# Order of the first statistics and the queues of the last table writes in the preparation of a two-layer metaformer kernel

## The chip, the cores and the metric

The kernel runs on one core of a Trainium2 chip. The metric is the device time of one execution in microseconds (us), as the median over runs. The profile is of one further execution.

## What is computed

The input `x` has shape (4, 256, 64, 64), float32. Two layers follow one another, and each adds a convolution branch and then a recurrent branch to `x`:

```python
x = x + dcnv2(ln_c(x), w_off, b_off, w_conv)   # layer 0: 27 offset/mask maps by a 3x3 convolution,
                                               # 9 bilinear samples per pixel, 256x256 weights per tap
t = t + lstm(ln_t(t), ...)                     # along the 4096 tokens, four gates, h and c of 256
x = x + channel_gate(ln_c(x), ...)             # layer 1: x times a sigmoid gate per image and channel
t = t + lstm(ln_t(t), ...)                     # same recurrence with other weights
```

The deformable convolution reads the normalized image at data-dependent places. The kernel serves these reads from a table in DRAM, whose entry for a pixel place holds neighbouring pixels, so that one indirect DMA fetches the corners of 128 samples.

## The kernel before, in words

Everything is float32. A tile is `[128 partitions, 256 channels]`: 4 images times 32 rows of pixels, for one column and one parity of the row (even or odd). There are 128 such tiles, 64 columns times two parities. The on-chip array `ring` takes the even tiles of the preparation and `squares` the odd ones; both hold 40 tiles.

**Preparation** (`prepare`, line 91). The 64 columns are worked in N = 17 groups: one of 2 columns, three of 4, one of 3, one of 5, ten of 4 and a last one of 2. For each group `g`:

- `load` fetches the raw tiles of `x` (groups 0 to 2 through the queues of SyncE and ScalarE, the others through GpSimd's, lines 330 to 335 and 370);
- `stats(g)` computes mean and variance on VectorE (`bn_stats`, then `norm_of`, a Newton iteration of small dependent instructions);
- `norm` normalizes in place on ScalarE;
- `to_table(g)` (line 275) writes the normalized tiles to the DRAM table. For each parity there are four DMAs, one for each image. Before the change the even half (`table<-ring`) is issued by SyncE and the odd half (`table<-squares`) by GpSimd;
- `turned` transposes on TensorE, `taps` and `offsets` make the offset convolution, and `samples` on VectorE turns the offsets into a **plan**: the addresses and the four weights of every sample, kept in DRAM in 16 pieces of 180 KB by GpSimd (`keep`).

`offsets` uses the matrices `from_above` and `from_below`, which are copies of the identity shifted by one row. Before the change they are made in `metaformer_kernel` (lines 1773 to 1778), outside the hand-written order. From group 3 on one weight load (an "errand": `wconv`, then `Us`, `Vs`, `bs` of each gate) goes to SyncE's queue for each group.

**Order.** The class `Ordered` (line 409) wraps an engine so that its instructions keep program order on that engine. All of its instructions show as L420, the helper's line. What is issued through the plain `tc.nc` is placed by the scheduler of the build. Each queue works its instructions in order: a DMA whose data is ready still waits behind the one issued before it on the same engine.

**Sampling and first recurrence** (`sample_and_recur`, line 571). `plan_of` (line 608) fetches a piece of the plan through SyncE's queue when it is first needed (`used<-plan`). `gather` (line 616) issues the indirect DMAs through GpSimd (`squares<-table,used`), 1,152 in all. A gather depends on its plan piece and on the whole table. ScalarE scales the first corner, VectorE adds the other three, TensorE transposes and multiplies with `wconv` (`acc`). From slot 38 of this loop on, the steps of the first recurrence are interleaved with it by a planner with fixed costs. `fetch` (line 686) brings `x` back into `ring` through SyncE's queue.

The first two plan pieces that are read are pieces 14 and 15, since the order starts with the odd tiles of columns 48 to 63; they are written early in the preparation. The class `Gate` (line 1350) makes some accumulators at its start (`gmx`, `lanes`, `own`, lines 1362 to 1370). The second recurrence (`gated_lstm`) follows with the gate between.

Of the kernel before, what the change touches and what calls it, by code (L numbers as in the profile page):

```python
# [11 lines left out]
F32 = mybir.dt.float32  # L12
# [7 lines left out]
P = 128  # L20
B, C, H, W = 4, 256, 64, 64
# [9 lines left out]
R = H // 2  # L31
# [59 lines left out]
def prepare(tc, pools, const, wts_, x_in, table, errands):  # L91
# [3 lines left out]
    after = pools["after"]  # L95
    nc = Ordered(tc.nc, after)
    ident, from_above, from_below = const
# [20 lines left out]
    plan = pools["dram"].tile([NTILE // OC, P, 5, OC, K], F32, name="plan")  # L118
# [104 lines left out]
    N = len(groups)  # L223
# [17 lines left out]
    def columns(e, g, lo, hi):  # L241
        return cols[e][:, at[g] + lo : at[g] + hi]
# [32 lines left out]
    def to_table(g):  # L275

        c, n = groups[g]
        lo, hi = int(g == 0), n + more[g]
        for e, engine in enumerate((nc.sync, nc.gpsimd)):
            if c + n == W:  # L280
                nc.gpsimd.memset(columns(e, g, n, n + 1), 0.0)
            if g == 0:
                nc.gpsimd.tensor_copy(again[:, e], columns(e, 0, 0, 1)[:, 0])
            elif at[g] == 1:
                last = groups[g - 1][1] + more[g - 1]
                nc.gpsimd.tensor_copy(columns(e, g, -1, 0), columns(e, g - 1, last - 1, last))
            if g == N - 1:
                nc.gpsimd.tensor_copy(columns(e, g, n, n + 1)[:, 0], again[:, e])
            for i in range(B):
                rows = tabs[i, :, 1 + e : 1 + H : 2].rearrange("x y c -> y x c")  # L290
                own = columns(e, g, lo - 1, hi)[i * R : (i + 1) * R]
                both = bass.AP(own.tensor, own.offset, [own.ap[0], [C, hi - lo], [1, 2 * C]])
                engine.dma_start(rows[:, c + lo : c + hi], both)
# [44 lines left out]
    stats(0)  # L338
    norm(0, 4)
    to_table(0)  # L340
    xt = turned(*(columns(e, 0, 0, 1)[:, 0] for e in range(2)))
    stats(1)
    stats(2)
# [227 lines left out]
def sample_and_recur(  # L571
# [12 lines left out]
    nc = Ordered(tc.nc, pools["after"])  # L584
# [23 lines left out]
    def plan_of(c):  # L608
        if c not in chunk:
            chunk[c] = stp.tile([P, 5, OC, K], F32, name=f"used{c}", tag="used", bufs=3)  # L610
            nc.sync.dma_start(chunk[c], plan[c])
        return chunk[c]

    rounds = {}
# [735 lines left out]
class Gate:  # L1350
# [3 lines left out]
    def __init__(self, tc, pools, const, params):  # L1354
        self.tc, self.pools, self.const, self.params = tc, pools, const, params
        kp = pools["keep"]
        nc = tc.nc
        self.low = kp.tile([P, NTILE], F32, name="glow", tag="glow")
        self.rs = kp.tile([P, NTILE], F32, name="grs", tag="grs")

        self.mx = kp.tile([P, 2, C], F32, name="gmx", tag="gmx")
        nc.vector.memset(self.mx, -3.0e38)

        self.lanes = kp.tile([P, 2, 2, C], F32, name="lanes", tag="lanes")
        nc.vector.memset(self.lanes, 0.0)
        self.pq = None

        self.own = kp.tile([P, B], F32, name="own", tag="own")
        ident = const[0]
        nc.vector.tensor_reduce(self.own, ident.rearrange("p (i r) -> p i r", i=B), AX.X, ALU.add)  # L1370
# [364 lines left out]
@with_exitstack  # L1735
def metaformer_kernel(ctx: ExitStack, tc: tile.TileContext, a: dict, out: bass.AP):
    nc = tc.nc
    fp = ctx.enter_context(tc.tile_pool(name="flag", bufs=1))
    dr = ctx.enter_context(tc.tile_pool(name="dram", bufs=1, space=DRAM))

    cnt = fp.tile([P, 2, 2], F32, name="cnt")
    x1 = dr.tile([P, NTILE, C], F32, name="x1d")
    x2 = dr.tile([P, NTILE, C], F32, name="x2d")
    ffn = [[[a[f"L{layer}_ffn_{kind}_{g}"] for g in "ioc"] for kind in "UVb"] for layer in range(2)]
    gate = [a[f"L1_conv_{n}"] for n in ("w", "gamma", "beta", "running_mean", "running_var")]

    with ExitStack() as main:

        def pool(name, bufs, space=None):
            kw = {} if space is None else {"space": space}  # L1750
            return main.enter_context(tc.tile_pool(name=name, bufs=bufs, **kw))

        cp = pool("const", 1)
        pools = {
            "chunk": pool("chunk", 2),
            "v": pool("v", 4),
            "small": pool("small", 2),
            "state": pool("state", 1),
            "cm": pool("cm", 6),
            "y": pool("y", 2),  # L1760
            "keep": pool("keep", 1),
            "median": pool("median", 1),
            "dram": dr,
            "tr": pool("tr", 2, PSUM),
            "acc": pool("acc", 2, PSUM),
            "misc": pool("misc", 1, PSUM),
            "ga": pool("ga", 1, PSUM),
            "gb": pool("gb", 1, PSUM),
        }
        ident = cp.tile([P, P], F32, name="ident")  # L1770
        make_identity(nc, ident)

        from_above = cp.tile([P, P], F32, name="from_above")
        nc.vector.tensor_copy(from_above[:, 1:], ident[:, : P - 1])
        nc.vector.memset(from_above.rearrange("p (i r) -> p i r", i=B)[:, :, 0:1], 0.0)
        from_below = cp.tile([P, P], F32, name="from_below")
        nc.vector.tensor_copy(from_below[:, : P - 1], ident[:, 1:])
        nc.vector.memset(from_below.rearrange("p (i r) -> p i r", i=B)[:, :, R - 1 : R], 0.0)
        const = (ident, from_above, from_below)
        pools["ring"] = cp.tile([P, RING, C], F32, name="ring")  # L1780

        pools["squares"] = cp.tile([P, RING, C], F32, name="squares")
        pools["numbers"] = lambda table: table.rearrange("e (c a) -> (e c) a", a=1)
        pools["after"] = InOrder(tc)

        woff = cp.tile([P, NC, K * NOM], F32, name="woff")
        pools["w_off"] = a["w_off"].rearrange("(n p) k o -> p n (k o)", p=P)
        bias = cp.tile([P, NOM], F32, name="bias")
        nc.sync.dma_start(bias, a["b_off"].rearrange("(a o) -> a o", a=1).to_broadcast([P, NOM]))
        wconv = cp.tile([P, NC, K, C], F32, name="wconv")  # L1790
        table = dr.tile([B * NENT, 2 * C], F32, name="table")
        w_conv = a["w_conv"].rearrange("(n p) k o -> p n k o", p=P)
        errands = [[lambda nc: nc.sync.dma_start(wconv, w_conv)], []]
        weights = [lstm_weights(nc, cp, *ffn[n], tag=n, errands=errands[n]) for n in range(2)]
        plan, rest = prepare(
            tc, pools, const, (woff, bias, (a["grid"], a["first"])), a["x"], table, errands[0]
        )
        ws = cp.tile([P, NC, 3], F32, name="ws")
        nc.sync.dma_start(ws, gate[0].rearrange("(k p) u -> p k u", p=P))
        vec = []  # L1800
        for name, v in zip(("gamma", "beta", "rmean", "rvar"), gate[1:]):
            t = cp.tile([P, NC], F32, name=name)
            with nc.allow_non_contiguous_dma(reason="256 numbers"):
                nc.sync.dma_start(t, v.rearrange("(k p) -> p k", p=P))
            vec.append(t)
        gamma, beta, rmean, rvar = vec
        nc.vector.tensor_scalar(rvar, rvar, 1e-5, None, ALU.add)
        scale = cp.tile([P, NC], F32, name="scale")
        nc.vector.tensor_mul(scale, gamma, inv_sqrt(nc, pools["small"], rvar, NC))
        gt = Gate(tc, pools, const, (ws, scale, rmean, beta))  # L1810
        held = sample_and_recur(
            tc, pools, const, wconv, a["x"], table, plan, x1, x2, weights[0], cnt[:, 0], gt, rest, errands[1]
        )
        gated_lstm(tc, pools, const, weights[1], x2, out, cnt[:, 1], gt.gates(held))


    held = fp.tile([P, 1], F32, name="held")
    nc.vector.tensor_reduce(held, cnt.rearrange("p l i -> p (l i)"), AX.X, ALU.add)
    bad = fp.tile([P, 1], F32, name="bad")
    all_held = 4.0 * NC * B * (R - 1)  # L1820
    nc.vector.tensor_scalar(bad, held, all_held - 0.5, None, ALU.is_lt)
    anybad = fp.tile([P, 1], F32, name="anybad")
    nc.gpsimd.partition_all_reduce(anybad, bad, P, bass_isa.ReduceOp.max)
    flag = fp.tile([P, 1], I32, name="flag")
    nc.vector.tensor_copy(flag, anybad)
    again = nc.values_load(flag[0:1, 0:1], min_val=0, max_val=1)
    with tc.If(again > 0):
        in_order(tc, x1, out, ffn, gate)
# [53 lines left out]
```

## Time and profile before

| | |
|---|---|
| three runs | 3296.19, 3307.12, 3334.37 us, median 3307.12 |
| profiled execution | 3307.03 us, span 3305.2 us, 0.967 of the TensorE clock granted |
| busy over the span | PE 93%, DVE 79%, ACT 62%, POOL 49% |
| first table write on SyncE's queue | issued at 19.96 us |
| last table write on SyncE's queue | issued at 189.95 us |
| first gather on GpSimd | issued at 195.30 us |
| first multiplication with `wconv` | 208.77 us |

PE is TensorE's matmul, PEld its weight load, DVE VectorE, ACT ScalarE, POOL GpSimd. SPq, ACTq and POOLq are queues of DMA issues. In a row of the timeline the columns are start and duration in us, engine, line, operation, written tile, read tiles, shape and number of merged instructions; in brackets stands the idle time before it and what ended it. A row of the table of windows gives the stretch and its length, then the busy time of each engine with the number of instructions, the granted clock, the busy share of the 16 DMA engines, and GB/s.

### The profile page before, as it was taken

To read this page: it belongs to the slowest core of one execution; us is meant where nothing else is said; L and a number is where in the kernel's file an instruction comes from. 1 tells how busy PE (TensorE), PEld (TensorE's weight loads), DVE (VectorE), ACT (ScalarE), POOL (GpSimd) and SP (SyncE) were. 2 spreads that over 40 slices of the span, in tenths; PEclk is the share of its full clock that TensorE was granted. 3 is DMA by queue.
4 is the path that set the end of the run, shared out by engine and by line. 5 is a ranking of instruction groups with operands and counts; after the bars stand their busy time and mean duration, and the time that the engine had idled before them with its cause. 6 is when DMAs were issued, how large, how long until landed. Compare 5 with 4: busy or idle time off the path is not lost.

```text
span 3305.2 us, 61505 instructions
## 1 busy us (share of the span) xinstructions
PE 3060.9 (93%) x20382; PEld 2837.9 (86%) x20382; DVE 2622.9 (79%) x7456; ACT 2058.2 (62%) x5446; POOL 1619.8 (49%) x1583
## 2 busy tenths in 40 slices
PE   7956899999999999999999999999894999999998
PEld 6945788898898889999899899988883999999997
DVE  6656778787898889989889889987576677777774
ACT  5734555565676666766676666766774666666663
POOL 3357566666676666766666756664000022222221
PEclk9978999999999999999999999999996999999999
DMA  9997888898889889999899899886102144544442
GB/s 297 332 310 286 296 301 301 287 322 309 320 301 330 302 292 334 322 323 327 306 321 337 294 328 331 309 315 243 49 27 83 56 134 147 153 151 151 150 141 85
DMA packets 317351, 826.57 MB, mean 250 GB/s; under 512 B 104472, under 2 KB 109976, under 8 KB 312160
## 3 DMA queue, kind: packets, MB, share of 16 engines
q0 software_dynamic: 188416, 669.68, 58.2%
q1 hardware_dynamic: 128464, 152.60, 13.8%
q8 instruction: 164, 2.69, 0.3%
q14 instruction: 163, 1.34, 0.1%
q10 hardware_dynamic: 144, 0.26, 0.0%
HBM read 701.46 MB, written 120.94 MB: 249 GB/s over the span
## 4 chain that ended last, share of the span: by engine, by line
PE 79%; issue 9%; ACT 4%; DVE 3%; another core or an unknown queue 2%; DMA 1%; SPq 1%; POOL 0%; ACTq 0%; DVEq 0%; POOLq 0%
PE acc L420 27%; PE ga L420 12%; PE gacc L420 7%; PE gtr L420 7%; PE tr L420 7%; PE gb L420 6%; PE ggb L420 4%; PE gga L420 4%; ACT v L420 1%; PE zacc L420 1%; DMA squares<-table,used 1%; DVE v L420 1%; PE xt L420 1%; PE zga L420 1%
## 5 line engine op out<-in xcount | busy, mean ns | idle before, releaser
L420 POOL DMA_INDIRECT squares<-table,used x1152 | 1373.3, 1192 | 733.4 <-issue 168.5
L420 DVE SCALAR_TENSOR_TENSOR v<-squares,used,v 128x256 f32<-128x256 f32 x3456 | 1412.7, 477 | 132.8 <-ACT v L420 95.6
L420 PE MATMUL acc<-wconv,vt 128*128 128x256 f32 x4608 | 1125.4, 388 | 86.8 <-ACT vt L420 61.5
L420 PEld LDWEIGHTS acc<-wconv,vt 128*128 128x128 f32 x4608 | 849.5, 195 | 194.7 <-ACT vt L420 68.2
L420 ACT COPY vt<-tr 128x512 f32<-128x512 f32 x576 | 335.7, 583 | 710.2 <-PE tr L420 514.0
L420 ACT ACTIVATE v<-squares,used 128x256 f32<-128x256 f32 x1152 | 528.8, 512 | 67.4 <-DMA squares<-table,used 56.9
L420 PE MATMUL tr<-ident,v 128*128 128x128 f32 x2304 | 352.4, 275 | 28.5 <-DVE v L420 23.0
L420 PEld LDWEIGHTS tr<-ident,v 128*128 128x128 f32 x2304 | 276.7, 142 | 44.1 <-DVE v L420 21.3
L420 DVE TENSOR_TENSOR tg<-tg,ti 128x256 f32<-128x256 f32 x284 | 119.9, 422 | 232.2 <-ACT ti L420 222.2
L420 PEld LDWEIGHTS ga<-cm,Us 128*128 128x128 f32 x2272 | 275.1, 193 | 24.8 <-ACT cm L420 16.8
L420 PE MATMUL ga<-cm,Us 128*128 128x128 f32 x2272 | 279.4, 276 | 14.1 <-ACT cm L420 12.4
L420 PEld LDWEIGHTS ga<-h,Vs 128*128 128x128 f32 x2256 | 278.4, 195 | 11.3 <-issue 4.7
L420 PE MATMUL ga<-h,Vs 128*128 128x128 f32 x2256 | 281.6, 278 | 3.7 <-issue 3.6
L420 POOL DMA_DIRECT2D hd<-sqh x60 | 34.8, 580 | 408.5 <-DVE sqh L420 388.0
L420 POOL DMA_DIRECT2D ring<-hd x240 | 144.4, 630 | 166.7 <-DMA hd<-sqh 152.7
L420 DVE TENSOR_TENSOR h<-to,th 128x256 f32<-128x256 f32 x282 | 119.1, 422 | 132.1 <-ACT th L420 118.6
L420 ACT ACTIVATE tg<-gacc,bs 128x128 f32<-128x128 f32 x284 | 88.7, 363 | 185.6 <-PE gacc L420 185.6
L420 PEld LDWEIGHTS gacc<-h,Vs 128*128 128x128 f32 x1128 | 147.5, 192 | 14.7 <-DVE h L420 7.4
L420 PEld LDWEIGHTS gb<-h,Vs 128*128 128x128 f32 x1128 | 148.4, 193 | 10.5 <-issue 4.2
L420 PE MATMUL gacc<-h,Vs 128*128 128x128 f32 x1128 | 150.1, 276 | 6.2 <-DVE h L420 6.2
L420 PEld LDWEIGHTS gb<-cm,Us 128*128 128x128 f32 x1136 | 147.6, 192 | 9.3 <-issue 1.9
L420 PE MATMUL gb<-h,Vs 128*128 128x128 f32 x1128 | 150.8, 276 | 3.7 <-issue 3.7
(219 smaller groups left out, 4551.4 us busy)
## 6 DMA issues: line engine op xcount, KB each, us to landing
squares<-table,used POOLq DMA_INDIRECT x1152
ring<-x2d SPq DMA_DIRECT2D x18, 1024.0 KB
ring<-in_x_dram SPq DMA_DIRECT2D x65, 256.0 KB
x1d<-ring SPq DMA_DIRECT2D x64, 256.0 KB
x2d<-ring SPq DMA_DIRECT2D x16, 1024.0 KB
xd<-sqx SPq DMA_DIRECT2D x64, 256.0 KB
cm<-xd SPq DMA_DIRECT2D x256, 64.0 KB
out_dram<-ring SPq DMA_DIRECT2D x32, 512.0 KB
```

What stands on the lines that cost most here:

```text
L420: ins = op(*args, **kw)
```

## The change

It has four parts, all at the preparation or right after it.

1. In `prepare`, the shifted copies of the identity are made after `stats(0)`, `norm(0, 4)` and `to_table(0)`, inside the hand-written order.
2. In `to_table`, the even half of the last three groups (14, 15, 16) is issued by GpSimd in place of SyncE. These are 12 DMAs.
3. In `plan_of`, the first two plan pieces are fetched through ScalarE's queue in place of SyncE's.
4. In `Gate`, the accumulators at its start join the hand-written order, which puts them after the preparation's VectorE work.

```diff
@@ to_table
-        for e, engine in enumerate((nc.sync, nc.gpsimd)):
+        for e, engine in enumerate((nc.sync if g < N - 3 else nc.gpsimd, nc.gpsimd)):
@@ prepare
     stats(0)
     norm(0, 4)
     to_table(0)
+
+    nc.vector.tensor_copy(from_above[:, 1:], ident[:, : P - 1])
+    nc.vector.memset(from_above.rearrange("p (i r) -> p i r", i=B)[:, :, 0:1], 0.0)
+    nc.vector.tensor_copy(from_below[:, : P - 1], ident[:, 1:])
+    nc.vector.memset(from_below.rearrange("p (i r) -> p i r", i=B)[:, :, R - 1 : R], 0.0)
     xt = turned(*(columns(e, 0, 0, 1)[:, 0] for e in range(2)))
@@ plan_of
-            nc.sync.dma_start(chunk[c], plan[c])
+            (nc.sync if len(chunk) > 2 else nc.scalar).dma_start(chunk[c], plan[c])
@@ Gate.__init__
-        nc = tc.nc
+        nc = Ordered(tc.nc, pools["after"])
@@ metaformer_kernel
-        from_above = cp.tile([P, P], F32, name="from_above")
-        nc.vector.tensor_copy(from_above[:, 1:], ident[:, : P - 1])
-        ...
-        nc.vector.memset(from_below.rearrange("p (i r) -> p i r", i=B)[:, :, R - 1 : R], 0.0)
+        from_above, from_below = (cp.tile([P, P], F32, name=n) for n in ("from_above", "from_below"))
```

More of the change, by code (lines that the diff above doesn't have):

```diff
@@ L1771, in metaformer_kernel @@
         make_identity(nc, ident)
-        from_above = cp.tile([P, P], F32, name="from_above")
[L1774 to L1777, printed above, removed]
-        nc.vector.memset(from_below.rearrange("p (i r) -> p i r", i=B)[:, :, R - 1 : R], 0.0)
+        from_above, from_below = (cp.tile([P, P], F32, name=n) for n in ("from_above", "from_below"))
         const = (ident, from_above, from_below)
```

## The prediction, made before the changed kernel was run

> **What bounds the kernel now.** I read the page first, for the chain that ended last, then the table of windows over the preparation and after it, then the timeline of VectorE at the start and of the two DMA-issuing queues at the end. All parts of the change lie before 196 us, so I need what bounds that stretch and whether a gain there lasts.
>
> ```profile
> PE 79%; issue 9%; ACT 4%; DVE 3%; another core or an unknown queue 2%; DMA 1%; SPq 1%; POOL 0%; ACTq 0%; DVEq 0%; POOLq 0%
> ```
>
> SPq is 1% of the chain: about 33 us at most can be had from SyncE's queue.
>
> ```profile
> 15.00:35.00 20.00, 12.40 (x44) 9.24 (x44) 18.99 (x95) 9.05 (x19) 9.08 (x19) 0.91 1.00 378
> 35.00:80.00 45.00, 43.70 (x271) 40.45 (x272) 28.72 (x110) 34.10 (x72) 15.17 (x29) 1.00 0.92 257
> 80.00:155.00 75.00, 75.00 (x469) 69.82 (x468) 55.48 (x225) 54.34 (x113) 26.84 (x49) 1.00 1.01 336
> 155.00:195.00 40.00, 28.48 (x180) 26.42 (x178) 17.83 (x63) 15.32 (x33) 9.60 (x18) 0.91 0.95 272
> 200.00:220.00 20.00, 12.02 (x51) 9.50 (x52) 14.93 (x36) 8.49 (x17) 15.43 (x18) 0.70 1.01 379
> ```
>
> The last two columns are the DMA share and GB/s. Two things are full at once: the matmul row (75.00 of 75 us from 80 to 155) and the 16 DMA engines (1.01). In 35 to 80 and 155 to 195 the DMA engines have a little idle time and move fewer bytes per us. After 200 they are full again, with gathers.
>
> ```profile
> 13.05 0.28 POOL masks.py:199 TENSOR_SCALAR_AFFINE_SELECT ident<-ident 128x128 f32<-128x128 f32 x1 [9.91 <-issue]
> ...
> 13.36 0.23 DVE L1774 COPY from_above<-ident 128x127 f32<-128x127 f32 x1 [10.88 <-POOL ident masks.py:199]
> ...
> 13.86 0.42 DVE L420 BATCH_NORM_STATS2 st<-ring 128x6 f32<-128x256 f32 x1
> ```
>
> The identity is late, its copies come first on VectorE, and the first statistics stand behind them. ScalarE's first wait ended on a load of `ring` at 7.33, so the data of group 0 is there about then.
>
> ```profile
> 171.19 1.74 SPq L420 DMA_DIRECT2D bs<-in_L_ffn_b_c_dram  x1
> 173.03 17.69 SPq L420 DMA_DIRECT2D table<-ring  x12
> 190.82 1.72 SPq L420 DMA_DIRECT2D used<-plan  x2
> 192.64 1.86 SPq L420 DMA_DIRECT2D ring<-in_x_dram  x4
> ```
> ```profile
> 156.00 2.24 POOL L420 DMA_DIRECT2D table<-squares  x4 [4.67 <-ACT squares L420]
> 165.66 2.17 POOL L420 DMA_DIRECT2D table<-squares  x4 [7.42 <-ACT squares L420]
> ...
> 175.13 2.21 POOL L420 DMA_DIRECT2D table<-squares  x4 [5.46 <-issue]
> 178.80 1.14 POOL L420 DMA_DIRECT2D plan<-made  x2 [1.46 <-DVE z L420]
> 195.30 1.08 POOL L420 DMA_INDIRECT squares<-table,used  x1 [15.36 <-DMA ring<-in_x_dram]
> ```
>
> `bs` is the last errand (group 12), so the 12 writes behind it are exactly the even halves of groups 14 to 16. SyncE starts group 14 at 173.03; GpSimd issued the odd half of the same group at 156.00. SyncE is 17 us behind, the plan pieces stand behind its 12 writes, and the first gather starts 2.76 us after the second plan issue ends (190.82 + 1.72 = 192.54).
>
> **What the skill says.** The Trainium skill, "DMA: Bandwidth & Descriptors", section "Queues, rings and completion order": each DMA engine takes turns between the queues that have work, packet by packet, and SP and ACT each own a queue. Section "Issuing engines are not separate DMA queues": DMAs from any engine share the same 16 engines, and spreading them saves only issue time. The trace agrees: at 1.01 share a further queue has no free engine to use. So most of SyncE's 17 us lag is backlog of full DMA engines, and moving the 12 writes moves the backlog. Section "Anatomy of one DMA — SWDGE (gpsimd) path": completion of a write to HBM costs most of some 2 us. No row here isolates it.
>
> **The change part by part**, against the profiled execution (3307.03 us; span 3305.2 and 1.8 around it; its time is within 0.1 us of the median 3307.12).
>
> *First statistics ahead.* Group 0's chain takes VectorE 13.86 to 18.31, 4.4 us. Started at 7.4 it ends at 11.8. Then the copies wait for the identity (13.34) and take what they took, 13.36 to 13.93. `stats(1)` starts at 13.95, not 18.23: 4.3 us earlier. TensorE's first transpose (19.05 before) needs identity and data and goes at about 13.4. VectorE is busy from 13.86 to 33.4 without a gap, so TensorE's closed chain, which begins at 35.10, begins at 30.8. But the gathers need the whole table, and its last bytes leave when the DMA engines have moved all of it. Earlier work helps there only by idle time that it fills. Idle of the DMA engines in 35 to 80: 8% of 45 = 3.6 us. From 80 to 155 there is none to win. I take -3.0; ends 0 and -3.6.
>
> *Twelve writes through GpSimd.* Issue: 12 x 0.55 us (the 2.21/4 of its own rows) = 6.6 us, hidden in GpSimd's idle (9.6 busy of 40 us from 155 to 195). The even half is normalized one ScalarE instruction ahead of the odd, so it goes out just before it. Behind these writes on GpSimd stand `plan<-made` and the gathers; plan pieces 14 and 15 are long written, so only the gathers matter, and these need the writes anyway. SyncE then runs dry after group 13, and its four fetches of `x` (1 MB) and the two plan pieces (0.36 MB) move before the last table write instead of after it. They use DMA time either way. What is won is idle: 5% of 40 us (155 to 195) = 2.0, and 8% of 195 to 200 = 0.4, so -2.4, of which I take -1.9. A new gap between the last landing and the first gather's bytes, which the fetches filled before: +1.5 (a gather's issue is 1.08; ends +0.5 and +2.5). And the rate: the tail moves 272 GB/s, 10.9 MB in 40 us, where two fed queues move 336 in the middle. At 336 it takes 32.4 us, -7.6; nothing shows how much of this is a lone SyncE queue and how much is that writes alone are slow (257 in 35 to 80, with both queues fed). I take -2, a quarter; ends 0 and -7.6.
>
> *Plan pieces through ScalarE.* Two issues of some 0.4 us (its one DMA issue at 0.75 took 0.40) after ScalarE's last sigmoid (184.35, so 180.0 shifted). Behind them is `scale(0)`, which waits for a gather. They land before the last table write, so the wait that ends last becomes the table. 0 on its own: its gain is inside the tail above. If the table were ready sooner it would be worth up to 195.30 - 190.7 = 4.6.
>
> *Gate's three.* 0.48 + 0.91 + 0.28 = 1.7 us from VectorE's idle start to about 185. VectorE idles from 189.9 to 200.88, so 0; 1.7 without that cover.
>
> Sum: -3.0 - 1.9 + 1.5 - 2.0 = -5.4, so 3307.0 - 5.4 = 3301.6, say **3302**. It lasts: until slot 38 of the sampling the gathers fill the DMA engines (1.01), then the matmul chain follows with fixed work, so the end moves with the first gather.
>
> **Rivals.** *A, the lag was the queue's and not the engines'.* For it: 1.5 us for each SyncE write against 0.55 for GpSimd's, and the low rate while SyncE is alone. Against: a share of 0.95. Then the full rate in the tail (-7.6), all idle (-3.6, -2.4) and the small gap: -3.6 - 2.4 - 7.6 + 0.5 = -13: 3294.
> *B, the full DMA engines swallow the head start.* For it: 1.01 over 75 us. Then 0 - 1.9 + 1.5: 3307, no change.
> *C, slower: the moved writes drain slower.* One queue with 2.8 MB more at the end and nothing but writes: in 50 to 55, with writes alone, the engines moved 219 GB/s. At 219 the tail's 10.9 MB take 49.7 us, +9.7; with -3.0 - 1.9 + 1.5 that is +6.3: 3313. It decides below 10.9 MB / 43.4 us = 251 GB/s. GpSimd's writes also wait for their own earlier DMAs (8.4 us in 11 waits before 260 us), and twice as many writes for each group would wait more.
> *That it doesn't do what it says*: the scheduler of the build could still place the identity's copies first. The order is written into the chain, so I count it within B.
>
> **Chances.** The forecast 0.55, A 0.15, B 0.2, C 0.1. Three runs before spread from 3296 to 3334, so a median after may stray by some 10 us whatever the change does. The cases give 3294 to 3313, but the ends are the unlikely ones; 3299 to 3307 with the stray of runs on both sides gives 3286 to 3320. A measurement can tell about 1% (33 us) from no change; no case reaches it. What is left for both sides is stray and a mechanism that I don't see: faster 0.04, same 0.92, slower 0.04.
>
> **What would show it.** `stats(1)` at about 14 and the first `acc` multiplication some 5 us before 208.77. SyncE ends its table writes near 169, then fetches `x`; GpSimd issues the last table writes before 176. First gather at 189 to 193, right after the last table write lands. The DMA share in 35 to 80 rises from 0.92 toward 0.98 if the head start is used. Wrong: a first gather later than 195, or table landings that follow GpSimd's issues at once (A: gather before 187).

## The result, and the profile after

Over 20 runs of each, the changed kernel takes 3306.61 us (median; 3295.00 to 3330.67) and the kernel before 3311.93 (3289.95 to 3334.37). The ratio is 0.9992 with an interval of 0.997 to 1.0014: no difference that these runs can tell. The profiled execution of after took 3302.81 us with a span of 3301.0, where before had 3305.2.

The chain of waits on the page has lost the 1% of SyncE's queue, and its share of DMA waits has gone from 1% to 3%:

```profile
PE 78%; issue 9%; ACT 4%; DMA 3%; DVE 3%; another core or an unknown queue 2%; POOL 0%; POOLq 0%; ACTq 0%; DVEq 0%
```

The timeline of the start. The statistics of group 0 (`st` at 6.88) now run as soon as their data is there, and the copies wait for the identity behind them. The identity itself came 1.03 us later than before (14.08 against 13.05), so `stats(1)` starts at 14.93 and not at 14 (in a later profile of after, with the identity at 13.08, it starts at 13.93):

```profile
6.88 0.43 DVE L425 BATCH_NORM_STATS2 st<-ring 128x6 f32<-128x256 f32 x1 [6.88 <-DMA ring<-in_x_dram]
...
14.08 0.28 POOL masks.py:199 TENSOR_SCALAR_AFFINE_SELECT ident<-ident 128x128 f32<-128x128 f32 x1 [10.95 <-issue]
...
14.39 0.23 DVE L425 COPY from_above<-ident 128x127 f32<-128x127 f32 x1 [3.14 <-POOL ident masks.py:199]
...
14.93 0.42 DVE L425 BATCH_NORM_STATS2 st<-ring 128x6 f32<-128x256 f32 x1
```

The table of windows over the same stretches, with three short ones around the first gather (the last two columns are DMA share and GB/s):

```profile
35.00:80.00 45.00, 43.79 (x275) 40.50 (x275) 31.40 (x119) 33.80 (x70) 16.44 (x31) 1.00 0.96 296
80.00:155.00 75.00, 75.00 (x469) 69.84 (x468) 55.49 (x224) 53.84 (x112) 28.56 (x52) 1.00 1.01 329
155.00:195.00 40.00, 24.75 (x158) 23.02 (x156) 16.23 (x56) 12.40 (x27) 15.77 (x28) 0.87 0.88 271
185.00:190.00 5.00, 0.00 (x0) 0.00 (x0) 2.70 (x9) 0.00 (x0) 0.55 (x1) 0.50 0.93 336
190.00:195.00 5.00, 0.00 (x0) 0.00 (x0) 0.00 (x0) 0.00 (x0) 1.50 (x2) 0.50 0.16 55
195.00:200.00 5.00, 0.00 (x0) 0.00 (x0) 0.48 (x1) 0.68 (x2) 3.78 (x5) 0.50 0.95 294
200.00:220.00 20.00, 13.80 (x56) 10.75 (x56) 16.44 (x40) 8.37 (x17) 15.73 (x17) 0.70 1.00 381
```

The same three short windows before:

```profile
185.00:190.00 5.00, 0.00 (x0) 0.00 (x0) 4.63 (x17) 0.00 (x0) 0.00 (x0) 0.81 0.93 273
190.00:195.00 5.00, 0.00 (x0) 0.00 (x0) 0.00 (x0) 0.00 (x0) 0.00 (x0) 0.50 0.90 261
195.00:200.00 5.00, 0.00 (x0) 0.00 (x0) 0.00 (x0) 0.00 (x0) 3.78 (x4) 0.50 0.92 311
```

From 35 to 80 more bytes move (296 GB/s, not 257). From 190 to 195 the DMA engines now nearly stand still (0.16, not 0.90). Added up over 185 to 200 they are idle for 5 x (0.07 + 0.84 + 0.05) = 4.8 us, where before it was 5 x (0.07 + 0.10 + 0.08) = 1.25.

The timeline of the issuing queues at the end of the preparation:

```profile
171.71 1.93 SPq L425 DMA_DIRECT2D bs<-in_L_ffn_b_c_dram  x1
173.74 9.05 SPq L425 DMA_DIRECT2D ring<-in_x_dram  x4
182.34 2.12 ACTq L425 DMA_DIRECT2D used<-plan  x2
```
```profile
151.78 1.66 POOL L425 DMA_DIRECT2D table<-ring  x3 [3.19 <-ACT ring L425]
...
173.97 1.71 POOL L425 DMA_DIRECT2D table<-ring  x3 [0.29 <-POOL ring L425]
176.15 0.55 POOL L425 DMA_DIRECT2D table<-ring  x1 [0.47 <-DMA table<-squares]
...
180.66 2.21 POOL L425 DMA_DIRECT2D table<-squares  x4 [3.56 <-issue]
184.41 1.14 POOL L425 DMA_DIRECT2D plan<-made  x2 [1.53 <-DVE m L425]
193.20 1.08 POOL L425 DMA_INDIRECT squares<-table,used  x1 [7.65 <-issue]
```

SyncE fetches `x` from 173.74, ahead of the last table writes. GpSimd issues its last four writes at 180.66, and then waits. The semaphores of the trace say for what. The last of these writes lands at 191.91, and the gather starts 1.29 us later, at 193.20. Before, the last write landed at 193.68, the plan piece at 194.24, and the gather followed 1.06 us after the piece. So the first gather is 2.1 us earlier: 1.77 by the table's landing, 0.56 because the piece no longer ends the wait, and 0.23 lost on the longer of the two delays.

The even half of group 14, which SyncE issued at 173.03 before, is now issued by GpSimd at 151.78. It goes out 21 us earlier, and the last landing comes 1.8 us earlier. So nearly all of SyncE's lag was the backlog of the full DMA engines, as the prediction had it, and not its queue's own.

### The profile page after: what moved, and what is told of

The parts are those of the page before. It is cut to its first block, busy times and chain, and to the rows that moved or that the text cites. A ratio compares the mean times of both kernels' runs of the same rounds, so it can differ in the third digit from the quotient of the medians.

```text
span 3301.0 us, 61504 instructions
## 1 busy us (share of the span) xinstructions
PE 3063.1 (93%) x20382; PEld 2838.5 (86%) x20382; DVE 2622.0 (79%) x7456; ACT 2056.4 (62%) x5446; POOL 1616.9 (49%) x1595
## 4 chain that ended last, share of the span: by engine, by line
PE 78%; issue 9%; ACT 4%; DMA 3%; DVE 3%; another core or an unknown queue 2%; POOL 0%; POOLq 0%; ACTq 0%; DVEq 0%
PE acc L425 27%; PE ga L425 12%; PE gacc L425 7%; PE gtr L425 7%; PE tr L425 7%; PE gb L425 6%; PE ggb L425 4%; PE gga L425 4%; DMA squares<-table,used 2%; ACT v L425 1%; PE zacc L425 1%; PE xt L425 1%; PE ht L425 1%; DMA table<-squares 1%
## 5 line engine op out<-in xcount | busy, mean ns | idle before, releaser
L425 PEld LDWEIGHTS ga<-h,Vs 128*128 128x128 f32 x2256 | 277.5, 195 | 10.3 <-issue 3.6
L425 PE MATMUL gb<-cm,Us 128*128 128x128 f32 x1136 | 152.5, 276 | 6.5 <-issue 5.2
```

The costliest lines, as they stand in the source:

```text
L425: ins = op(*args, **kw)
```

## The experiments

Theory: the gain is the head start, and the moved DMAs give part of it back. Rivals: A, the lag was SyncE's queue's own (the moved writes do it); B, the full DMA engines swallow the head start. "First gather" is the start of GpSimd's first `squares<-table,used`, "MB by 80" what the DMA engines had moved 80 us into the span. The runs come from three chips: the kernel before took 3282.64 us (one run) beside the first four kernels, 3344.95 (one run) beside the next four and 3180.26 (11 runs, 3175.17 to 3183.25) beside the last four. Single times therefore say little, and what I compare is the preparation, which is steadier: two profiles of before, whose times are 29 us apart, have their first gather at 195.30 and 195.47.

**The head start alone** (parts 1 and 4 of the change), twice:

```
-for e, engine in enumerate((nc.sync if g < N - 3 else nc.gpsimd, nc.gpsimd)):
+for e, engine in enumerate((nc.sync, nc.gpsimd)):
-            (nc.sync if len(chunk) > 2 else nc.scalar).dma_start(chunk[c], plan[c])
+            nc.sync.dma_start(chunk[c], plan[c])
```

> Only the first statistics ahead of the identity's copies, with the gate's three set-up instructions in order; table writes and plan pieces as before. Theory 1 (the DMA engines' backlog decides, and the earlier work fills their idle time between 35 and 80 us): TensorE leaves the preparation near 179.5, the last table write lands near 191 (193.68 before, 191.91 with the whole change), the first gather issues at 192 to 193 (195.30 before, 193.20 after). Rival B (full engines swallow the head start): TensorE also leaves near 179.5, but the first gather stays at 195 within 0.5 us.

> First statistics ahead alone, once more. Theory 1: 24.6 to 26.4 MB by 80 us; first gather 1 to 3 us earlier than in the repeat of the changed kernel, with 59.9 MB by then and no idle stretch, since the fetches of x fill it. Rival (the queue edits help): first gather later than in the repeat of the changed kernel.

**The queues alone** (parts 2 and 3 on the kernel before), twice; the edit is the reverse of this one, made to the kernel before.

> Only the two queue edits: the twelve writes through GpSimd, the first two plan pieces through ScalarE; first statistics as before. Theory 1: the plan pieces no longer land last (they cost 0.56 us before), and the writes keep their landing within 1 us, so the first gather issues at 194 to 195.5, and TensorE leaves the preparation at 183.2 as before. Rival A (the lag was SyncE's queue): first gather below 192.

> The queue edits alone, once more. Theory 1: 23.2 to 23.7 MB by 80 us, first gather 1 to 4 us later than in the repeat of the kernel before (198.83 against 195.30 in the first profiles), 60.5 MB by then, an idle stretch before it. Rival (the queue edits help): first gather earlier than in the repeat of the kernel before.

**Both kernels again**, for the spread; the changed one a third time in the last group:

> The kernel before once more, to see how far one profile strays. Theory 1 (bytes moved): by 80 us the DMA engines have moved 23.2 to 23.7 MB (23.48 in the first profile), the first gather issues at 195.3 within 2 us, and 59.8 MB have been moved by then. Rival (the profiles differ by chance alone): the bytes by 80 us lie anywhere between 23 and 26.5.

> The changed kernel once more. Theory 1: 24.6 to 26.4 MB by 80 us, first gather at 193.2 within 3 us with 60.5 MB moved by then, and a stretch of 3 us or more before it in which the DMA engines are nearly idle. Rival (chance alone): bytes by 80 us like those of the kernel before.

> Third profile of the changed kernel, unedited, for the spread: first gather at 187 to 194, 1.29 us after the last landing of a table write, and a DMA share of 0.1 to 0.3 in the 3 us ahead of it.

Measured, with the start of GpSimd's affine select that makes the identity, TensorE's last matmul of the preparation, and the GB/s of the tail from 155 to 185:

| kernel | single time | identity | TensorE's last | first gather | MB by 80 | tail GB/s |
|---|---|---|---|---|---|---|
| before, twice | 3307.03, 3335.63 | 13.05, 13.01 | 183.21, 183.21 | 195.30, 195.47 | 23.48, 23.61 | 274, 280 |
| head start alone, twice | 3297.19, 3347.96 | 13.63, 14.34 | 179.08, 180.01 | 191.75, 194.98 | 25.14, 24.50 | 276, 264 |
| queues alone, twice | 3300.99, 3339.11 | 13.87, 14.62 | 184.15, 184.77 | 198.83, 197.67 | 23.20, 23.51 | 282, 279 |
| after, three times | 3302.81, 3326.92, 3178.09 | 14.08, 13.38, 13.08 | 179.48, 178.82, 178.49 | 193.20, 189.89, 193.88 | 24.89, 25.35, 24.93 | 296, 312, 297 |

The identity comes at another time in each execution, 13.08 to 14.08 in the three of after alone, and TensorE follows it. From the identity to TensorE's last matmul it is 170.2 us without the head start (170.16, 170.20, 170.28, 170.15) and 165.4 to 165.8 in all ten profiles with it: the head start moves TensorE by 4.7 us, and the rest of the scatter there is the identity's. Whether the edits have a part in the later identity can't be told from two profiles of before.

What follows: every kernel with the head start has moved more than before by 80 us, 0.8 MB at least. Counted from the identity, each of them also has its first gather earlier (174.2 to 180.8 us after it, against 182.3 and 182.5 in before; the run with dead time, below, left out). So B falls. The queues alone make the first gather later, by 3.5 and 2.2 us, although the even half of group 14 goes out 17 us earlier there (156.45 in the first profile, not 173.03), so A falls as the cause of a gain. Counted from the identity, the first gather comes 182.4 us after it in before, 184.0 with the queues alone, 179.4 with the head start alone and 178.8 in after (means; the single ones stray by up to 2.3 us from them). So the head start gives some 3.0 us, and the queues take 1.6 alone and give 0.6 on top of it. With two or three profiles each, the sign of the head start is shown and its size is known to a microsecond or two; an effect of the queues on top of it isn't shown.

Several of the expectations missed. The queues alone were first put at 194 to 195.5. The second profile of the head start alone was to be 1 to 3 us ahead of the changed kernel beside it and is 5.1 behind (194.98 and 189.89), as the rival there had it; over all profiles that advantage is the 0.6 us above. The second profile of after is just ahead of its range, without the nearly idle stretch (a DMA share of 0.46 in the last 3 us), and in its third a plan piece ended the wait, not a table write.

Why the queues alone lose shows in their windows just ahead of the first gather (198.83 in this kernel):

```profile
195.00:198.80 3.80, 0.00 (x0) 0.00 (x0) 0.00 (x0) 0.00 (x0) 0.00 (x0) 0.50 0.27 107
198.80:200.00 1.20, 0.00 (x0) 0.00 (x0) 0.00 (x0) 0.00 (x0) 1.08 (x1) 0.50 0.00 0
```

The engines run dry while GpSimd waits, since the fetches that used to fill this place had gone ahead. By its first gather this kernel had moved 60.53 MB, before 59.77: the fetches put 0.76 MB ahead of the gathers, 2.7 us at the tail's 282 GB/s.

**The fetches behind the gathers** (the changed kernel, its first four fetches of `x` issued by GpSimd behind the first gathers), twice:

```
-            nc.sync.dma_start(place(n, 2), x_in[:, ORDER[n] : ORDER[n] + 2])
+            (nc.gpsimd if p < 4 else nc.sync).dma_start(place(n, 2), x_in[:, ORDER[n] : ORDER[n] + 2])
```

> The changed kernel with the first four fetches of x (1 MB) through GpSimd, behind the first gathers, where in the changed kernel they run on SyncE's queue beside the last table writes. Theory 1 (they share the engines with the table writes): the last table write lands up to 2.7 us earlier[...], first gather near 190.5 to 192; but the bytes only move behind it, so the 20th gather is at 220 within 1.5 us (220.43 after). Rival (the last landing hangs on something else): first gather at 193.2 within 0.5.

> Second profile of the changed kernel with its first four fetches of x behind the first gathers. If the fetches' 0.76 MB, moved ahead of the last table write, cost 2.7 us at the first gather, it is some 2 to 3 us earlier than in the changed kernel's own profile of this call, with the same megabytes moved by 80 us; if what sets it is how fast the engines happened to be, the difference follows the megabytes by 80 us, about 3 us for each.

Measured: first gather 194.51 and 187.29, 3304.96 and 3177.93 us. The first is a miss: 1.3 us later than after's 193.20 with the same identity (13.99), and 283 GB/s in its tail, not 296. The second is 6.6 us ahead of the unedited kernel beside it (193.88), with 0.5 MB more by 80. The mean of the two, 2.6 us earlier, is of the size that the put-off bytes should give (59.49 MB moved by the first gather and not 60.52: 1.03 MB, 3.5 us at after's 296 GB/s), but two so far apart don't prove it. Nor does the lead of the second last: it is 3.5 us at the 40th gather, 6.4 at the 76th, 1.8 at the 200th and 0.55 at the end of the span. That fits fetches which had only been put off while the engines were full (1.02 from 200 to 220), but one pair that wanders so much doesn't show it.

**The plan pieces.** First with all of them on SyncE in the changed kernel, then with ScalarE's queue for the first two but the table writes on SyncE as before:

```
-            (nc.sync if len(chunk) > 2 else nc.scalar).dma_start(chunk[c], plan[c])
+            nc.sync.dma_start(chunk[c], plan[c])
```

> The changed kernel with all plan pieces on SyncE's queue again. SyncE's queue holds nothing of the last three groups here, so the pieces are issued near 173.7 in front of the four fetches. Theory 1: the table's last landing still decides, first gather at 193.2 within 1 us. Rival (ScalarE's queue carries the gain): first gather back at 195 or later.

```
-for e, engine in enumerate((nc.sync if g < N - 3 else nc.gpsimd, nc.gpsimd)):
+for e, engine in enumerate((nc.sync, nc.gpsimd)):
```

> The changed kernel with the table writes on SyncE's queue as before: head start and plan pieces through ScalarE's queue alone. If the plan piece was the last wait of the first-only kernel by about 0.56 us and no more, the first gather comes 1.29 us after the last table landing and stands within 1 us of the first-only kernels (191.75 and 194.98); the fetches of x are issued behind the last table write again, so the DMA share right before the first gather stays above 0.5 instead of 0.13 to 0.16. If the early first gathers (187.7 to 193.2) of the changed kernel need the writes on GpSimd's queue, this one is at 192 to 195; if they came from the plan pieces, it is at 188 to 191.

Measured: with all on SyncE, 3291.36 us; the pieces are issued from 165.49 on, earlier than expected, and land at 177.2 and 179.4, the last table write at 186.39, and the gather starts 1.29 us after it, at 187.68. Once the writes are off SyncE's queue the pieces need no other queue. That it is 5 us earlier than after, far out of the expected range, goes with the most bytes of all (26.39 MB by 80), so it can't be put down to the edit. With the writes on SyncE, 3173.96 us and a first gather at 192.44, between the two of head start alone. ScalarE's queue doesn't get its pieces through early there, as the timeline of its end shows:

```profile
179.86 6.78 SPq L425 DMA_DIRECT2D table<-ring  x7
186.74 2.50 SPq L425 DMA_DIRECT2D ring<-in_x_dram  x4
186.77 1.31 ACTq L425 DMA_DIRECT2D used<-plan  x2
192.44 1.08 POOL L425 DMA_INDIRECT squares<-table,used  x1 [16.61 <-DMA ring<-in_x_dram]
```

ScalarE issues at 186.77, right after a write of SyncE's on the same semaphore landed (186.75); its second piece follows in the same way (187.76 after 187.68). So it looks as if a DMA here waits for its turn on a semaphore, behind an earlier one, whichever queue issued that. The first piece lands at 191.05, 1.7 us after the last table write (189.34), so here the piece ended the wait, against the expectation. The share of the DMA engines ahead of the gather is 0.90 and 0.76 here (185 to 190 and 190 to 195), as expected, since the fetches fill the place again.

**Does it last?** Dead time right ahead of the first gather:

```
     begin()
+    dead = pools["keep"].tile([P, 512], F32, name="dead", tag="dead")
+    for _ in range(48):
+        nc.gpsimd.memset(dead, 0.0)
```

> The changed kernel with 48 GpSimd fills of a 128x512 tile that nobody reads, right ahead of the first gather: about 30 us of dead time at the place where the lead of 2 to 6 us appears. Theory 1 (the end moves with the first gather): first gather at about 190 + 30 = 220 to 225, and the ratio to the kernel before is 1.008 (+27 us), interval within 1.005 to 1.011. Theory 2 (the sampling phase takes a few us in, the chain of matmuls does not care): first gather equally late, ratio 0.997 to 1.003. In between, say 1.004, half of a lead survives.

Measured: ratio to before 1.0059, interval 1.0046 to 1.0073 (3198.49 us against 3180.26). The timeline of GpSimd:

```profile
183.22 27.88 POOL L425 MEMSET dead<- 128x512 f32 x48
211.96 1.08 POOL L425 DMA_INDIRECT squares<-table,used  x1 [0.85 <-issue]
```

The fills took 27.88 us but began at 183.22, under the wait for the landings, so the first gather is 18.1 us behind that of the unedited kernel beside it (193.88) and not 30. From there nothing of it is won back: 18.3 us behind at the 40th gather, 16.1 at the 76th, 19.8 at the 200th, 20.9 at the last, 20.8 at the end of the span. In time it is 0.59% of 3180.26 = 18.8 us (14.6 to 23.2) over before, for a first gather 16.6 us later than the 195.4 of before's two profiles, which are from other executions. So a delay of 18 us at the first gather comes out whole at the end, to within the 3 us by which these differences wander. That a lead of 2 to 4 us does so too, if no work has been put off to get it, is inferred: it is too small for these runs to show.

## Why the prediction was right, and where its terms were off

The forecast was 3302, no change that can be measured; 3306.61 lies within its range, and the profiled span fell by 4.1 us where the sum said 5.4. Neither says much for the sum. The range of 3286 to 3320 also holds the times of all three rivals (3294 to 3313). That the 4.1 comes near is luck: single profiles stray by as much, and terms of the sum missed in opposite directions. The head start did what was forecast. The queue terms (-1.9, +1.5 and -2.0, together -2.4) did not: they measured +1.6 alone and -0.6, less than the stray, on top of the head start.

- *First statistics ahead, -3.0: the size came out, its reason only in part.* TensorE leaves the preparation 4.7 us earlier for the same identity (I had 4.3), and the first gather 3.0. The ten profiles with the head start have moved 25.07 MB by 80 us in the mean (24.43 to 26.39), before 23.55. That is 1.5 MB, 4.5 us at the 336 GB/s of the middle. The full stretch gives some back: by 155 us they are 1.2 MB ahead, 3.5 us. I had named idle time of the engines as the source. The share rose only from 0.92 to 0.96, 1.8 us; more of it is that more bytes move in a busy microsecond (296 GB/s, not 257). What makes them move faster was not tried.
- *New gap, +1.5: too small.* It measured 4.8 - 1.25 = 3.5 us, beyond my upper end of 2.5. I had counted a gather's issue (1.08), but ahead of it lie 1.29 us from landing to start and the time in which few of the 16 engines still work. A table write lands in 16 parts (16 updates of its semaphore), and the parts of the last table write come far apart when GpSimd issues it: in after from 187.33 to 191.91, 4.6 us, in all nine profiles with the moved writes 1.7 to 4.7 us. In the five profiles in which SyncE issues it they come within 1.2 to 1.4 us. The early fetches alone don't explain this: with the fetches behind the gathers the spread is still 4.5 and 1.7 us. What does was not tried. The Trainium skill, "DMA: Bandwidth & Descriptors", section "Queues, rings and completion order", has each engine take its own turns between queues; this trace fits that in so far as the parts of one DMA finish apart and the DMA is as late as its last part.
- *Idle won, -1.9, and rate, -2.0.* The idle time isn't won, it moved into the gap. The rate rose, in after's three profiles, from 274 to 296 to 312 GB/s, but not with the queues alone (282, 279). After's mean, 302, less before's, 277, over 30 us is 0.75 MB, about what the early fetches cost. Why it takes the head start for this stays open.
- *Plan pieces, 0: right in sum, wrong in its reason.* "They land before the last table write" held in after by 0.5 us, and failed in its third profile (192.82 against 191.85) and with the writes on SyncE.
- *Gate, 0.* Nothing in the profiles speaks against it; it ran only together with the head start.
- *"It lasts": right for a delay of 18 us*, which came out whole at the end, and not shown for a lead of this size. The two first profiles alone would have misled: the lead of after is 1.8 us at the 20th gather, 10.3 at the 40th, 12 at the 76th, -0.7 at the 1000th and 4.1 at the end of the span. The step between the 20th and the 40th is one stalled gather of before, shown in the last section.
- *The signs named ahead.* `stats(1)` near 14 held for an identity at the old time, and the DMA share from 35 to 80 rose, to 0.96. The first gather (193.20) is at the edge of 189 to 193. The first multiplication with `wconv` came at 206.96, 1.8 us earlier and not 5. GpSimd issued its last table write at 182.34 and not before 176: its waits for its own earlier writes of `table<-squares` grew from 8.4 us (11 waits) to 13.0 (17), as rival C had feared.

Rival B failed on the bytes moved by 80 us and on the first gather, A on the queues alone, C on the tail's rate: with the moved writes it was 279 GB/s or more from 155 to 185, and 258 or more from 155 to 195 with the gap in it, never its 251. C's conclusion, a loss from the moved DMAs, holds for the queues alone, by the late last parts, the gap and the early fetches in place of a lower rate. What stays open is the true size at the end. The runs leave -0.3% to +0.14%, and the 3 to 4 us at the first gather are 0.1%.

## What to carry to other kernels

With full DMA engines, look at what has to land before the next stage can start, and what the engines have to do while that is waited for: a transfer put ahead costs its bytes at once, and leaves a hole where it used to fill the wait, and the last parts of the last writes can come late, as GpSimd's did here. An early start is worth the extra bytes that move by the time the engines are full, not the microseconds by which the first instruction moved. Single profiles of one kernel differ by 4 us in their first gather: an edit of that size is measured from the event that starts its chain (here the identity), over repeats, or made larger.

## What the runs showed of the hardware

- From the last landing to the start of the first gather it took 1.29 us where a table write came last (seven profiles) and 1.06 to 1.39 where a plan piece did (six).
- The 16 parts of the last table write landed within 1.2 to 1.4 us where SyncE had issued it (five profiles) and within 1.7 to 4.7 us where GpSimd had (nine).
- A gather's issue on GpSimd takes 0.94 us mostly, but a few take 5 to 10 (six of the 1,152 in before). Rows of the timeline of before:

```profile
295.60 11.97 DVE L420 SCALAR_TENSOR_TENSOR v<-squares,used,v 128x256 f32<-128x256 f32 x30
...
298.40 9.98 POOL L420 DMA_INDIRECT squares<-table,used  x1 [1.51 <-ACT vt L420]
```

VectorE runs 30 of these without a gap until 307.57, and the gather ends at 308.38. The DMA engines' share in its 9.98 us is 0.17. One of 8.80 us at 254.66, with no like in after until 288.80, is where before fell back between the 20th and the 40th gather. The Trainium skill, "SBUF — State Buffer", section "Who interferes with whom", says that a VectorE instruction with two SBUF inputs contends with a GpSimd instruction that reads SBUF, and that the later one waits. This row fits, with the end of the gather 0.8 us behind the end of the run, but such a run of additions can't be the whole cause. In before, 50 gathers start with 4 us or more of a gapless run of them still to come; 43 of these are issued in under 1.3 us, and six take over 5. In the run from 250.28 the gather at 253.09 takes 1.27 us and the next one, at 254.66, takes 8.80. What holds up the few stays open; no run here took the additions away.
